# Dividing the softmax of an eight-head attention at the heads' outputs instead of at the probabilities

## The chip, the cores and the metric

The kernel runs on one core of one Trainium2 chip. A time is the device time of one execution in microseconds (us). The time before is the median of three runs; one more execution was recorded by the hardware profiler, and its rows and chains are what the text quotes. The engines are PE (TensorE: matmuls; its weight loads are listed as PEld), DVE (VectorE), ACT (ScalarE), POOL (GpSimd) and SP (SyncE, whose queue issues the DMAs here). Each takes its instructions in the order in which the program lists them, and waits at an instruction until what it needs is there.

## What is computed

64 graphs of 256 nodes with 256 features go through two layers. The first is two graph-attention steps, a layer norm, a feed-forward block of width 1024 with ReLU, and a second layer norm. The second layer is an attention with 8 heads of 32 features, a layer norm, a feed-forward block of width 1024 with GELU, and a layer norm. The change touches the attention of the second layer:

```python
scores = jnp.einsum('bhid,bhjd->bhij', q, k) / np.sqrt(dh)
attn = jax.nn.softmax(scores, axis=-1)
for r in range(Wv.shape[0]):          # R = 4 relations
    v_r = (src @ Wv[r] + bv[r])...    # per head
    mask = (adj_matrix == r)[:, None]
    out = out + jnp.einsum('bhij,bhjd->bhid', attn * mask, v_r)
attn_out = out.transpose(0, 2, 1, 3).reshape(Bb, Nn, Dm) @ Wo + bo
x = _ln(src + attn_out, g1, beta1)
```

The adjacency holds only zeros and ones, so two relations occur. The kernel uses the values of relation 0 for all pairs and the difference of the values of relation 1 and relation 0 for the pairs whose adjacency is one. All data is 32-bit floating point.

## The kernel before

Nothing of the 64 graphs is shared but the weights, which stay in SBUF. The work on one graph is cut into some 190 pieces, each a few instructions on one engine. Three lists written out in the source fix the order in which the program emits them: START, then PERIOD once per period (59 times), then END. An entry of PERIOD such as `A.dt13/3` means: piece A.dt13 of the graph that lies 3 behind the newest one. So six graphs are in work at a time, each in another stage, and each engine's stream is the list, filtered for its pieces. The scheduler of the framework is switched off for the five engines. It still adds the waits that the data and the buffers need.

The pieces that matter here, by their names in the lists. A letter ahead of the point is the stage: G graph attention, F first feed-forward and projections, A attention, T the tail with the second feed-forward.

- PE: G.wh0, G.wh1 (L747), G.eA, G.eB (L763), G.gA0, G.gA1 and G.gB (L800); F.ha to F.he and T.ha to T.he, the first product of each feed-forward block, done with seven products of blocks in place of eight (L661); F.f0, F.f1 (L686); T.fa to T.fe (L702), again seven products; F.q, F.k (L835); A.va to A.ve, the values (L848); A.sc0, A.sc1, the scores of four heads each (L880); A.o0, A.o1, the outputs of four heads each (L930); T.wo (L949).
- DVE: A.mx, the maxima of the scores (L887); A.rz, the reciprocals of the sums, 128x2 per head (L902); A.pm, the masked copy of the probabilities (L922); A.vk2, A.vk3 (L862), which take values out of PSUM and add a bias; G.away, the mask of the first layer, the first reader of the adjacency (L739); G.adA, G.adB, maxima in the first layer (L776 to L779); G.rzA, G.rzB, which divide the first layer's rows (L791, L794: whz); .ln, .nm and T.rbD, the layer norms (L502 to L538); F.hp1 to F.hp3 and T.hp1 to T.hp3, additions of PSUM to the hidden values (L637); T.fk1 to T.fk4 (L713) and T.fp1 to T.fp3 (L637), the same for the results.
- ACT: A.ex, the exponentials with their sums over a row (L894); G.wc, G.wd, G.lr, G.ex; F.r0 to F.r3 and T.ge0 to T.ge3, the activations (L678); F.qe, F.ke; A.vk1, A.vk4; A.oc0, A.oc1, which copy the outputs of four heads each from PSUM to oT and add the bias of the values (L941).
- POOL: A.sp, two scalings per head, of the probabilities by the reciprocals (L907); .ra and .rb, the weighted residuals (L554, L561); F.sA, F.sB, T.sC, sums of blocks for the seven products, and T.u0 to T.u3 (L584); .rs, the roots of the variances (L514).
- SP: L.xT, L.adj, L.x load a graph; T.out stores one.

A 32-bit tile is turned (transposed) in three steps, eleven times per graph: for each of eight heads' probabilities and for three layer norms. `.dt` is a transpose by DMA of the tile seen as 16-bit halves (L469, into one of two `pairs` buffers). `.dm` is two DMAs that bring the halves of the words together (L477, into one of two `halves` buffers). Then a copy joins the halves to words again (L484): `A.mg` for a head, F.cA, F.cB and T.cC for the norms. Of the eight joins of the heads POOL does the first head of each group of four, ACT does the other six, and ACT does the three of the norms. A new `.dt` waits until the `.dm` two turns back has landed, and a new `.dm` waits until the join two turns back has read its buffer.

So one head goes this way: scores on PE; maximum on DVE; exponentials and sums on ACT; reciprocal on DVE; scaling on POOL; transpose and halves by DMA; join on POOL or ACT; mask on DVE; outputs on PE:

```python
def over_sums(h):                                   # POOL, L904
    p = t["p", h]
    for i in range(NT):
        nc.gpsimd.tensor_scalar(
            p[:, :, :, i, :], p[:, :, :, i, :], t["rz", h][:, i : i + 1], 1.0,
            ALU.mult, ALU.mult,
        )
```

PSUM is handed out as eight banks of one kind to whoever comes next in the list. A second function, `general`, computes the same for adjacencies with other numbers; its instructions stand in the program behind a branch that these inputs don't take.

Of the kernel before, what the change touches and what calls it, by code (L numbers as in the profile page):

```python
# [25 lines left out]
F32 = mybir.dt.float32  # L26
U8 = mybir.dt.uint8
U16 = mybir.dt.uint16
# [6 lines left out]
P = 128  # L35
# [8 lines left out]
G.nmA/1 A.mx13/3 A.rz12/3 F.raB/4 F.sB/3 T.hk3/5 A.mx11/3 A.rz10/3 L.xT/0 T.hp3/5 A.vp2/4 A.dm02/4  # L44
A.pm03/4 G.wh0/0 A.mg02/4 T.hd/5 A.ex13/3 T.hp2/5 G.wh1/0 A.ex11/3 A.sp12/3 A.dm00/4 G.wc0/0
A.sp10/3 G.wc1/0 A.ve/4 A.pm01/4 F.dtA/1 A.mg00/4 F.dmA/1 F.f1/2 A.pm02/4 G.eA/0 A.pm00/4 T.rbC/5
F.rbB/4 A.vk4/4 T.he/5 T.ge0/5 A.rz11/3 A.pm11/4 A.rz13/3 A.dt10/3 F.lnB/2 A.sc0/3 A.o0/4 T.ge1/5
A.mx00/3 G.lrA/0 F.cA/1 T.hk4/5 A.o1/4 T.ge2/5 A.sp11/3 A.sp13/3 A.mx02/3 A.dt12/3 F.ha/1 A.oc0/4
T.ge3/5 L.adj/0 A.oc1/4 F.sA/1 A.ex00/3 F.hb/1 A.mx03/3 G.away/0 A.dm10/3 A.dm12/3 F.rsB/2 F.hk1/1
F.hk2/1 T.wo/4 A.mx01/3 G.adA/0 A.mg10/3 T.u0/5 F.hp1/1 T.lnC/4 F.hc/1 T.u1/5 A.mg12/3 A.dt13/3  # L50
G.exA/0 F.raA/1 A.dt11/3 F.nmB/2 A.ex03/3 A.dm13/3 G.rzA/0 T.fa/5 F.hk3/1 A.ex02/3 T.rsC/4 T.fb/5
F.hd/1 T.nmC/4 G.gA0/0 T.u3/5 T.fk1/5 T.fk2/5 A.rz03/3 A.ex01/3 T.u2/5 F.hp2/1 L.x/0 F.hp3/1
A.mg13/3 A.sp03/3 G.gA1/0 A.pm12/3 G.wd0/0 G.wd1/0 A.dm11/3 A.rz01/3 T.fc/5 A.va/3 A.vb/3 F.dtB/2
T.fk3/5 A.mg11/3 F.rbA/1 A.sp01/3 F.r0/1 A.pm13/3 T.dtC/4 A.rz02/3 A.vk1/3 G.eB/0 T.fd/5 F.dmB/2
T.fp1/5 A.vk2/3 G.lrB/0 T.fp2/5 F.cB/2 F.he/1 A.vc/3 T.dmC/4 T.fe/5 A.rz00/3 F.r1/1 G.adB/0
A.dt03/3 T.cC/4 A.dt01/3 F.q/2 A.vk3/3 G.exB/0 F.hk4/1 A.vp3/3 T.fp3/5 F.qe0/2 F.k/2 A.sp02/3
T.fk4/5 F.r2/1 T.ha/4 F.qe1/2 A.dm03/3 F.ke0/2 T.hk1/4 T.lnD/5 G.rzB/0 T.nmD/5 A.sp00/3 T.sC/4
G.gB/0 A.vp1/3 T.hb/4 A.dm01/3 T.rsD/5 A.dt02/3 T.raC/4 F.ke1/2 T.rbD/5 T.hp1/4 A.sc1/2 T.out/5
A.dt00/3 G.lnA/0 A.mg03/3 T.hk2/4 F.r3/1 A.mg01/3 A.mx12/2 A.mx10/2 A.vd/3 G.rsA/0 T.hc/4 A.pm10/3
F.f0/1 A.ex12/2 A.ex10/2  # L60
# [5 lines left out]
G.away:0 L.adj:2 S.lw:0 S.v0:0 L.adj:1 G.wh0:0 G.wh1:0 G.wc0:0 G.wc1:0 G.eA:0 G.lrA:0 G.adA:0  # L66
S.f0:0 G.exA:0 G.rzA:0 G.gA0:0 G.gA1:0 G.wd0:0 G.wd1:0 S.f1:0 G.eB:0 G.lrB:0 S.f2:0 L.xT:1 G.wh1:1
G.adB:0 G.wh0:1 L.xT:2 G.exB:0 G.rzB:0 G.wc0:1 G.wc1:1 G.gB:0 G.wh0:2 G.eA:1 G.away:1 G.lrA:1
G.lnA:0 G.rsA:0 G.nmA:0 G.adA:1 F.dtA:0 F.raA:0 G.exA:1 S.p2:0 S.v1:0 G.wh1:2 S.q0:0 G.wc0:2
G.rzA:1 G.wc1:2 G.gA0:1 G.gA1:1 L.xT:3 G.eA:2 G.wd0:1 F.dmA:0 S.v2:0 S.q1:0 G.wd1:1 G.eB:1 F.cA:0  # L70
G.lrB:1 F.sA:0 G.adB:1 G.lrA:2 L.x:1 F.ha:0 S.lr:0 F.hk1:0 F.hb:0 G.away:2 G.adA:2 F.hk2:0 F.hc:0
F.hk3:0 F.hp3:0 F.hd:0 F.hp2:0 G.exB:1 F.he:0 F.r0:0 F.hp1:0 G.wh1:3 G.rzB:1 S.j1:0 G.gB:1 G.lnA:1
F.r1:0 F.hk4:0 F.r2:0 F.r3:0 G.wh0:3 F.f0:0 G.wc0:3 G.exA:2 L.adj:3 G.rsA:1 G.nmA:1 G.rzA:2 F.f1:0
G.gA0:2 F.rbA:0 G.gA1:2 F.lnB:0 G.wd0:2 L.x:2 L.xT:4 G.wc1:3 S.v3:0 G.wh1:4 G.wd1:2 F.rsB:0
F.dtA:1 F.dmA:1 G.eA:3 G.eB:2 G.lrB:2 F.cA:1 F.nmB:0 G.wh0:4 G.adB:2 G.lrA:3 F.ha:1 F.sA:1 G.exB:2
F.hb:1 F.dtB:0 F.hk1:1 F.raB:0 G.rzB:2 G.away:3 F.dmB:0 F.hk2:1 G.gB:2 G.lnA:2 G.wc0:4 F.cB:0
F.hc:1 F.k:0 G.adA:3 G.rsA:2 G.wc1:4 G.nmA:2 F.hk3:1 F.ke0:0 F.q:0 F.ke1:0 F.hp3:1 F.hd:1 F.qe0:0
L.x:3 F.hp1:1 F.hp2:1 F.qe1:0 F.r0:1 A.sc1:0 F.raA:1 A.mx13:0 F.he:1 A.mx10:0 F.r1:1 A.ex13:0
F.dtA:2 F.hk4:1 F.rbB:0 F.raA:2 F.r2:1 A.sc0:0 F.r3:1 A.rz13:0 A.mx12:0 A.mx00:0 A.sp13:0 F.dmA:2
G.exA:3 A.ex10:0 A.ex12:0 A.mx01:0 A.ex01:0 A.dt13:0 A.rz10:0 G.rzA:3 A.rz12:0 F.cA:2 F.sB:0  # L80
F.f0:1 F.f1:1 G.gA0:3 A.sp10:0 F.rbA:1 A.dm13:0 A.mx02:0 A.ex02:0 A.mg13:0 A.dt10:0 A.rz01:0
A.ex00:0 G.wd0:3 G.gA1:3 A.sp12:0 F.lnB:1 A.dt12:0 A.va:0 A.vb:0 A.mx11:0 G.wd1:3 A.sp01:0 F.rsB:1
A.vk1:0 G.eB:3 A.dm10:0 A.dm12:0 A.mg10:0 F.nmB:1 G.lrB:3 F.dtB:1 A.ex11:0 A.mg12:0 A.mx03:0
S.l0:0 F.ha:2 F.hk1:2 A.rz00:0 A.dt01:0 G.adB:3 A.pm10:0 A.rz11:0 F.sA:2 A.vk2:0 F.dmB:1 A.rz02:0
F.hb:2 F.hk2:2 A.dm01:0 A.vc:0 F.hc:2 A.ex03:0 S.l1:0 A.vk3:0 A.pm13:0 A.vd:0 F.cB:1 A.sp11:0
A.rz03:0 F.k:1 G.exB:3 A.vp1:0 F.hk3:2 A.mg01:0 A.sp02:0 F.ke0:1 F.hp1:2 G.rzB:3 F.hp3:2 F.q:1
A.dt11:0 F.rbA:2 A.vp2:0 F.ke1:1 F.hd:2 A.ve:0 F.qe0:1 F.qe1:1 A.dt02:0 A.dm11:0 A.sp00:0 F.hp2:2
G.gB:3 A.pm12:0 A.dm02:0 A.vk4:0 A.sp03:0 G.lnA:3 S.l2:0 A.mg11:0 F.he:2 F.r0:2 A.sc1:1 G.rsA:3
A.mx11:1 F.hk4:2 A.mg02:0 A.mx12:1 A.vp3:0 A.ex11:1 A.sc0:1 F.r1:2 A.dt03:0 A.rz11:1 A.mx13:1
# [1223 lines left out]
```

## Time and profile before

| what | us |
|---|---|
| runs | 3124.27, 3115.12, 3122.83 |
| median | 3122.83 |
| profiled execution, own time | 3121.47 |
| its span, first to last instruction | 3119.7 |
| busy PE, DVE, ACT, POOL | 3007.0, 2747.0, 2548.7, 2290.2 |

The profiled execution's own time holds 1.8 us around its span. The granted TensorE clock is 0.992 of full speed in the mean and 1.00 from 500 to 3000 us. The 16 DMA engines are busy for 0.71 of the steady stretch in the mean, and nearly all their packets come from SP's queue.

How to read the rows: a group of instructions is given by its line in the source, engine, operation, out<-in, shapes and count; then the time in which any of them ran, and the mean time of one in ns; then the engine's idle time just before them, and what ended it. Instructions of one engine overlap a little, so the sum of single times is more than the busy time. A matmul of 32-bit numbers is two instructions in the trace. A wait row reads: engine and tile that waited, what it waited for, us in total, times, longest. "SPq" is the queue of SP, whose time to issue a DMA isn't counted as busy.

### The profile page before, as it was taken

The page shows a single profiled execution, that of the slowest core. Times are in us where ns is not written, and L with a number is a line of the kernel's source. Part 1 is how long each engine was busy: PE and PEld are TensorE (multiplying, and loading weights), DVE is VectorE, ACT ScalarE, POOL GpSimd, SP SyncE. Part 2 cuts the span into 40 slices and gives each one's busy share as a digit, 9 for nine tenths or more (in the row PEclk, how much of TensorE's full clock was granted, in tenths as well). Part 3 has the DMA queues.
Part 4 walks back from the last instruction along what each step waited for, and adds up shares of the span by engine and source line. Part 5 has one row for each costly group of instructions (what it writes and reads, how often), then busy time and mean ns, then how long its engine had stood idle before and what let it go on. Part 6 is the DMA issues. An engine that isn't in the chain of part 4 may idle for free.

```text
span 3119.7 us, 68789 instructions
## 1 busy us (share of the span) xinstructions
PE 3007.0 (96%) x23270; PEld 2629.7 (84%) x23270; DVE 2747.0 (88%) x5744; ACT 2548.7 (82%) x5822; POOL 2290.2 (73%) x3057
## 2 busy tenths in 40 slices
PE   6899999999999999999999999999999999999986
PEld 5788888888888888888898888888888888888876
DVE  5689999899998899898999899999999999889965
ACT  2688888888888888888888888888888888878874
POOL 4568777777777777777777777777777777777765
PEclk9999999999999999999999999999999999999998
DMA  5577766677676777776676666677677776767663
GB/s 156 108 145 149 149 149 143 146 155 143 149 151 137 142 146 151 148 152 138 155 150 144 148 142 145 150 152 147 147 153 145 149 149 143 146 138 151 149 133 73
DMA packets 1023941, 449.41 MB, mean 144 GB/s; under 512 B 771008, under 2 KB 1021888, under 8 KB 1023584
## 3 DMA queue, kind: packets, MB, share of 16 engines
q1 hardware_dynamic: 1022320, 442.70, 67.9%
q8 instruction: 188, 3.08, 0.5%
q0 software_dynamic: 976, 1.72, 0.4%
q14 instruction: 169, 1.38, 0.2%
q10 hardware_dynamic: 288, 0.52, 0.1%
HBM read 58.87 MB, written 16.78 MB: 24 GB/s over the span
## 4 chain that ended last, share of the span: by engine, by line
PE 68%; DVE 12%; DMA 8%; issue 3%; ACT 3%; POOL 1%; SPq 1%; DVEq 0%; ACTq 0%; POOLq 0%
PE ff_a L686 11%; PE hX_c L661 6%; PE o L930 5%; PE fX_c L702 5%; PE hX_a L661 4%; PE sc L880 3%; PE q L835 3%; PE hY_c L661 3%; PE k L835 3%; PE gat_b L800 3%; PE vX L848 3%; PE wh L747 3%; DVE pm L922 2%; PE wo L949 2%; DMA adj<-in_adjT 2%
## 5 line engine op out<-in xcount | busy, mean ns | idle before, releaser
L484 ACT COPY pm<-halves_p 128x1024 uint16<-128x1024 uint16 x384 | 522.4, 1360 | 137.8 <-DMA halves_p<-pairs_p 135.7
L922 DVE TENSOR_TENSOR pm<-pm,adj 128x512 f32<-128x512 f32 x512 | 565.6, 1123 | 19.3 <-POOL pm L484 12.2
L686 PE MATMUL ff_a<-w_L_gnn_w_ff,hid_a 128*128 128x256 f32 x2048 | 463.0, 379 | 0.1
L686 PEld LDWEIGHTS ff_a<-w_L_gnn_w_ff,hid_a 128*128 128x128 f32 x2048 | 384.0, 190 | 50.4 <-ACT hid_a L678 0.8
L484 POOL COPY pm<-halves_p 128x1024 uint16<-128x1024 uint16 x128 | 180.2, 1408 | 157.5 <-DMA halves_p<-pairs_p 140.4
L930 PE MATMUL o<-pm,v 128*32 128x256 f32 x4096 | 235.3, 381 | 5.5 <-POOL p L907 2.4
L678 ACT ACTIVATE hid_a<-hid_a,col_L_gnn_b_ff 128x256 f32<-128x256 f32 x512 | 230.1, 500 | 3.3 <-DVE hid_a L637 3.2
L678 ACT ACTIVATE hid_c<-hid_c,col_L_gnn_b 128x256 f32<-128x256 f32 x512 | 224.4, 498 | 5.1 <-DVE hid_c L637 2.4
L930 PEld LDWEIGHTS o<-pm,v 128*32 128x32 f32 x4096 | 126.2, 110 | 104.6 <-issue 15.9
L702 PE MATMUL fX_c<-f_L_gnn_W,hid_c 128*128 128x128 f32 x1536 | 207.2, 278 | 7.3 <-ACT hid_c L678 5.1
L514 POOL TENSOR_TENSOR rstd_a<-var_a,neghalf 128x2 f32<-128x2 f32 x64 | 45.0, 702 | 222.5 <-DVE var_a L510 222.5
L702 PEld LDWEIGHTS fX_c<-f_L_gnn_W,hid_c 128*128 128x128 f32 x1536 | 192.8, 192 | 13.2 <-ACT hid_c L678 5.8
L661 PEld LDWEIGHTS hX_a<-cols_a,f_L_gnn_w_ff 128*128 128x128 f32 x1024 | 126.9, 195 | 33.1 <-ACT hid_c L678 22.2
L880 PE MATMUL sc<-kT,qT 32*128 32x256 f32 x2048 | 149.6, 400 | 3.3 <-ACT p L894 2.8
L584 POOL TENSOR_TENSOR S_c<-cols_c 128x128 f32<-128x128 f32 x128 | 58.3, 455 | 128.4 <-ACT cols_c L484 128.4
L800 PE MATMUL gat_a<-whz_A,s_A 128*128 128x258 f32 x512 | 134.9, 400 | 18.2 <-DVE whz_A L794 15.4
L661 PE MATMUL hX_a<-cols_a,f_L_gnn_w_ff 128*128 128x128 f32 x1024 | 144.6, 285 | 6.4 <-ACT cols_a L484 5.0
L747 PE MATMUL wh<-wx,xT 128*128 128x260 f32 x512 | 136.0, 390 | 12.5 <-DVE wx L372 10.1
L661 PEld LDWEIGHTS hX_c<-S_c,f_L_gnn_W 128*128 128x128 f32 x1024 | 134.0, 191 | 8.5 <-ACT hid_c L672 1.3
L702 PE MATMUL fY_c<-f_L_gnn_W,H_c 128*128 128x128 f32 x1024 | 137.3, 278 | 3.8 <-POOL H_c L584 3.8
L661 PE MATMUL hX_c<-cols_c,f_L_gnn_W 128*128 128x128 f32 x1024 | 135.8, 276 | 2.7 <-ACT cols_c L484 2.7
L661 PE MATMUL hX_a<-S_a,f_L_gnn_w_ff 128*128 128x128 f32 x1024 | 136.9, 277 | 0.0
(2760 smaller groups left out, 9808.9 us busy)
## 6 DMA issues: line engine op xcount, KB each, us to landing
halves_p<-pairs_p SPq DMA_DIRECT2D x1024, 128.0 KB, 3.3
xT<-in_xT SPq DMA_DIRECT2D x64, 256.0 KB, 3.4
adj<-in_adjT SPq DMA_DIRECT2D x64, 256.0 KB, 3.5
x<-in_x SPq DMA_DIRECT2D x64, 256.0 KB, 3.5
halves_y_a<-pairs_y_a SPq DMA_DIRECT2D x128, 128.0 KB, 3.0
halves_y_y<-pairs_y_y SPq DMA_DIRECT2D x128, 128.0 KB, 3.5
halves_y_c<-pairs_y_c SPq DMA_DIRECT2D x128, 128.0 KB, 3.2
out<-res_d SPq DMA_DIRECT2D x64, 256.0 KB, 2.6
```

The source lines that it names most:

```text
L484: copy(into().bitcast(U16).rearrange("p (n s) -> p s n", s=2), t["halves"].rearrange("p s k q -> p s (k q)"),)
L661: nc.tensor.matmul(ps[:, f * P : (f + 1) * P], weights()[0][:, factor, f * P : (f + 1) * P], left, start=start and f == 0, stop=f == FC // ...
L678: nc.scalar.activation(tiles["hid"][:, f, :], tiles["hid"][:, f, :], func, bias=b1[:, f : f + 1])
L686: nc.tensor.matmul(tiles["ff"][:, i, :], tiles["hid"][:, f, nodes(i)], weights()[2][:, f, :], start=(f == 0), stop=(f == FC - 1),)
L702: nc.tensor.matmul(ps, left[:, f, :], weights()[2][:, factor, f * P : (f + 1) * P], start=start and f == 0, stop=f == FC // 2 - 1, skip_gr ...
L747: nc.tensor.matmul(t["whp", j], tiles["xT"][:, c, nodes(j)], wx[:, c, :], start=(c == 0), stop=(c == KC - 1),)
L800: nc.tensor.matmul(ps, t["s"][:, j, nodes(i)], t["whz"][:, j, :width], start=(j == 0), stop=(j == NT - 1),)
L835: nc.tensor.matmul(t[key + "p"][:, o, :], w[:, c, nodes(o)], tiles["cols"][:, c, :], start=(c == 0), stop=(c == KC - 1),)
L848: nc.tensor.matmul(ps, left, wv[:, factor, :], start=start, stop=True, skip_group_check=True)
L880: nc.tensor.matmul(t["sc", g, hh][:, i, :], qkv["q"][hd, g, nodes(i)], qkv["k"][hd, g, :], start=True, stop=True,)
L922: nc.vector.tensor_tensor(pm[:, 1, :], pm[:, 0, :], tiles["adj"], ALU.mult)
L930: nc.tensor.matmul(ps[hh * DH : (hh + 1) * DH, :], qkv["v"][:, j, d0 : d0 + DH], t["pm", (g, hh)][:, r, j * N : (j + 1) * N], start=(r == ...
```

## The change

The probabilities stay undivided. They are turned, joined and masked as the exponentials come, and the outputs of the heads are multiplied by the reciprocals of the sums when they are taken out of PSUM. There the nodes lie along the free dimension, so the reciprocals are needed as rows, the same row in all 32 partitions of a head. They get there in five new pieces: A.iz (DVE) takes the reciprocals of all sums of a graph at once, four times side by side, so that a tile of 128x64 words, or 128x128 16-bit halves, is full; A.zt (SP) turns this tile by DMA; A.zd (SP) stores 32 of its rows in DRAM, 256 bytes each; A.zr (SP) reads them back in four DMAs, each spreading one row of 2 KB over 32 partitions; A.zj (ACT) joins the halves to words.

The pieces A.rz (DVE) and A.sp (POOL) are gone. A.oc0 and A.oc1 move from ACT to DVE and become a product with these rows. The bias of relation 0's values, which they added, is multiplied by the output weights once, in the setup (S.w1, four matmul instructions), and added to a bias row that is added to the residual anyway (S.w2). Four joins of heads instead of two are done on POOL. The buffers of p (the probabilities) become three instead of four, those of the first layer's scores s one instead of two. All three lists are new.

```diff
-t["z", h] = small.tile([P, NT], F32, tag="az", name=f"az_{b}_{g}{hh}", bufs=4)
-p = t["p", h] = work.tile([P, 2, NT, NT, 64], F32, tag="p", name=f"p_{b}_{g}{hh}", bufs=4)
+if "z" not in t:
+    t["z"] = small.tile([P, HG, HEADS // HG, NT], F32, tag="az", name=f"az_{b}", bufs=2)
+p = t["p", h] = work.tile([P, 2, NT, NT, 64], F32, tag="p", name=f"p_{b}_{g}{hh}", bufs=3)
...
-def inverse(h):
-    t["rz", h] = small.tile([P, NT], F32, tag="arz", name=f"arz_{b}_{h}", bufs=8)
-    nc.vector.reciprocal(t["rz", h], t["z", h])
...
+def inverses():
+    t["rz"] = small.tile([P, 4, HEADS * NT], F32, tag="arz", name=f"arz_{b}", bufs=1)
+    z = t["z"].rearrange("p h g i -> p (h g i)")
+    nc.vector.reciprocal(t["rz"], z.unsqueeze(1).to_broadcast([P, 4, HEADS * NT]))
+def turn_inverses():
+    t["zrow"] = work.tile([P, P], U16, tag="zrow", name=f"zrow_{b}", bufs=1)
+    nc.sync.dma_start_transpose(
+        out=t["zrow"], in_=t["rz"].rearrange("p a n -> p (a n)").bitcast(U16)
+    )
+def store_inverses():
+    t["flat"] = dram.tile([HG, 2 * HEADS // HG * NT, P], U16, tag="flat", name=f"flat_{b}", bufs=2)
+    nc.sync.dma_start(out=t["flat"].rearrange("h k q -> (h k) q"), in_=t["zrow"][: 2 * HEADS * NT])
+def spread_inverses():
+    t["zs"] = work.tile([P, HEADS // HG * NT, 2, P], U16, tag="zs", name=f"zs_{b}", bufs=1)
+    for hh in range(HG):
+        nc.sync.dma_start(
+            out=t["zs"][hh * DH : (hh + 1) * DH].rearrange("p k s q -> p (k s q)"),
+            in_=t["flat"][hh].rearrange("k q -> (k q)").partition_broadcast(DH),
+        )
+def join_inverses():
+    t["inv"] = work.tile([P, HEADS // HG, N], F32, tag="inv", name=f"inv_{b}", bufs=1)
...
+    copy(words.rearrange("p (k q s) -> p k s q", k=HEADS // HG * NT, s=2), t["zs"])
...
-nc.scalar.activation(
-    t["oT"][:, g, :], t["op", g], AF.Identity, bias=bv0[:, g : g + 1], scale=1.0
-)
+nc.vector.tensor_tensor(t["oT"][:, g, :], t["op", g], t["inv"][:, g, :], ALU.mult)
...
-    partial(both, h), "POOL" if hh in ((0,), (0,))[g] else "ACT",
+    partial(both, h), "POOL" if hh in ((0, 2), (0, 2))[g] else "ACT",
...
-s = t["s"] = work.tile([P, NT, N], F32, tag="s", name=f"s_{step}{b}", bufs=2)
+s = t["s"] = work.tile([P, NT, N], F32, tag="s", name=f"s_{step}{b}", bufs=1)
```

The new PERIOD, whose order the prediction walks through:

```
A.dm10/4 A.mg10/4 L.xT/0 A.zj/4 T.hp2/5 T.ge0/5 A.pm02/4 T.he/5 F.dmA/1 A.pm10/4 F.lnB/2 A.sc0/3
A.o0/4 T.raC/5 F.cA/1 A.mx10/3 A.o1/4 A.mx03/3 A.mx00/3 T.ge1/5 F.rsB/2 A.oc0/4 A.mx01/3 T.hk4/5
A.dt13/3 A.dt12/3 F.sA/1 T.rbC/5 G.wh0/0 T.ge2/5 L.adj/0 A.oc1/4 T.ge3/5 A.dm13/3 A.ex00/3
A.dm12/3 A.ex01/3 G.wh1/0 G.wc0/0 G.away/0 A.mg12/3 G.wc1/0 F.ha/1 G.eA/0 F.hb/1 A.dt11/3 T.u0/5
A.mx02/3 A.mg13/3 F.nmB/2 G.lrA/0 F.hk1/1 F.hk2/1 T.wo/4 A.ex03/3 A.dt00/3 G.adA/0 T.lnC/4
A.ex10/3 F.raB/3 G.exA/0 A.dm11/3 T.u1/5 A.dm00/3 T.fb/5 A.mg00/3 F.hc/1 T.fa/5 F.hk3/1 A.mg11/3
F.hd/1 G.rzA/0 A.dt03/3 F.hp3/1 F.dtB/2 A.ex02/3 T.fk1/5 F.hp1/1 G.gA0/0 T.rsC/4 G.gA1/0 G.wd0/0
T.nmC/4 A.dm03/3 G.wd1/0 T.fk2/5 A.va/3 F.dmB/2 T.fp1/5 A.vk1/3 A.vb/3 F.hp2/1 T.dtC/4 G.eB/0
T.u3/5 G.lrB/0 F.rbB/3 T.fc/5 A.iz/3 F.he/1 F.cB/2 A.mg03/3 A.vk2/3 T.fk3/5 T.u2/5 G.adB/0 F.raA/1
A.vc/3 T.fd/5 A.vp1/3 A.dt01/3 F.r0/1 L.x/0 T.fp2/5 G.exB/0 T.dmC/4 A.pm11/3 F.k/2 A.vk3/3 F.q/2
T.fe/5 F.hk4/1 A.zt/3 G.rzB/0 A.pm00/3 A.dm01/3 F.ke0/2 T.cC/4 F.ke1/2 F.r1/1 A.vd/3 A.vp3/3
F.r2/1 F.qe0/2 F.rbA/1 T.fp3/5 A.dt02/3 T.sC/4 T.fk4/5 A.zd/3 A.dt10/3 T.lnD/5 G.gB/0 F.qe1/2
A.vp2/3 T.ha/4 T.rsD/5 T.hb/4 A.ve/3 G.lnA/0 T.hk1/4 A.sc1/2 T.hk2/4 T.hc/4 F.r3/1 G.rsA/0 T.nmD/5
A.vk4/3 T.rbD/5 A.dm02/3 A.zr/3 G.nmA/0 A.mg01/3 F.sB/2 F.f0/1 A.mg02/3 A.mx13/2 A.ex13/2 T.hp1/4
T.hk3/4 T.hd/4 F.f1/1 A.mx12/2 A.mx11/2 T.out/5 A.pm03/3 A.pm13/3 A.pm01/3 A.ex12/2 A.ex11/2
F.dtA/0 A.pm12/3 T.hp3/4
```

In the old one the neighbours of the same places on DVE's and SP's side are: T.hp2 directly behind T.hd and ahead of A.pm01, A.pm02, A.pm00 and F.lnB; L.adj behind A.dt12; T.lnC, F.nmB and G.rzA between T.wo and G.gA0.

## The prediction

> **What bounds the kernel now.** I first read the busy times, then a steady stretch, the starts of one matmul group from graph to graph, the waits, and the rows of what the change touches.
>
> The page's busy times of the whole execution:
>
> ```profile
> PE 3007.0 (96%) x23270; PEld 2629.7 (84%) x23270; DVE 2747.0 (88%) x5744; ACT 2548.7 (82%) x5822; POOL 2290.2 (73%) x3057
> ```
>
> The same in the steady stretch, where start and end don't dilute it:
>
> ```profile
> core 0: us, PE busy (x) PEld busy (x) DVE busy (x) ACT busy (x) POOL busy (x), PEclk, DMA share, GB/s
> 200.00:2900.00 2700.00, 2661.89 (x20866) 2335.65 (x20856) 2469.22 (x5138) 2296.79 (x5246) 2035.74 (x2707) 1.00 0.71 147
> ```
>
> PE is busy for 98.6% of it, at the full clock. Two key groups of consecutive graphs, in the timeline of PE (start, duration):
>
> ```profile
> 1489.28 1.89 PE L835 MATMUL k<-cols_y,w_L_gnn_Wk 128*128 128x256 f32 x8
> 1534.94 1.89 PE L835 MATMUL k<-cols_y,w_L_gnn_Wk 128*128 128x256 f32 x8
> ```
>
> They lie 45.66 us apart. From graph 5 to 58 the distance is 46.90 us in the mean, and never under 45.66. Adding up PE's groups of one period, each by the shortest usual distance to the next group, gives 45.65: that is **PE's floor**, and a period loses 1.25 us over it. 2700 us are 57.6 periods, so per period PE is busy 46.2, DVE 42.9 (idle 4.0), ACT 39.9, POOL 35.4. DVE is the second bound. The waits (us in total, times, longest) say the same:
>
> ```profile
> DVE hid_c L637 <- PE hX_c L661: 68.9, 60, 3.0
> ...
> DVE away L739 <- DMA adj<-in_adjT: 64.3, 44, 3.6
> ...
> PE gat_a L800 <- DVE whz_A L794: 15.4, 25, 2.7
> ...
> PE fX_c L702 <- DVE acc_c L713: 12.0, 34, 1.1
> ```
>
> What PE waits for most in the steady state is DVE being late (whz, then the sums after it in DVE's order), and DVE is late because it waits twice a period, about 1.1 us each, for PE's hX_c and for the adjacency's landing.
>
> **The change, part by part.** The rows of what is moved:
>
> ```profile
> L484 ACT COPY pm<-halves_p 128x1024 uint16<-128x1024 uint16 x384 | 522.4, 1360 | 137.8 <-DMA halves_p<-pairs_p 135.7
> ...
> L484 POOL COPY pm<-halves_p 128x1024 uint16<-128x1024 uint16 x128 | 180.2, 1408 | 157.5 <-DMA halves_p<-pairs_p 140.4
> ...
> L941 ACT ACTIVATE oT<-o,col_bv 128x256 f32<-128x256 f32 x128 | 60.0, 471 | 46.5 <-PE o L930 46.0
> ```
>
> PE: the same matmuls per graph; four instructions once in the setup. The floor stays 45.65.
>
> POOL: 16 scalings of L907 go. They are 551.6 us in the stretch, 9.6 a period. Two joins come, 2 x 1.41. Net -6.8: 35.4 becomes 28.6. POOL sets no end, so this is worth nothing by itself; its cover was 11 us of spare time.
>
> ACT: two joins and two copies of the outputs go, the join of the inverses comes (1024 16-bit elements, as L484): -2 x 1.36 - 2 x 0.47 + 1.36 = -2.3. ACT has 7 us spare; nothing by itself.
>
> DVE: eight reciprocals go. L902 has 69.3 us for 460, 0.15 each, but in DVE's timeline the next instruction starts 0.07 later, so the gain is 0.6 to 1.2. Two products at the heads' outputs come; the nearest row is L862 (128x256, one side in PSUM), 0.41, so 0.8. One reciprocal of 128x64 comes, which no row shows: between 0.15 (128x2) and 0.68 (the maximum of 128x512, L887); I take 0.25, nearest to the 0.28 of 128x128 (L713). Sum -0.4 to +0.9, taken +0.3. Against it stands DVE's contention with POOL. DVE's timeline:
>
> ```profile
> 1362.68 4.04 DVE L922 TENSOR_TENSOR pm<-pm,adj 128x512 f32<-128x512 f32 x3
> 1366.65 0.15 DVE L902 RECIPROCAL arz_(1, 1)_16112<-az 128x2 f32<-128x2 f32 x1
> 1366.72 0.66 DVE L922 TENSOR_TENSOR pm<-pm,adj 128x512 f32<-128x512 f32 x1
> ```
>
> The three mask products of the first line take 1.35 each, with POOL in its additions L561 (in POOL's timeline from 1362.71 to 1366.18). The one of the last line takes 0.66; a scaling L907 starts beside it only at 1366.90. Another, which started after a scaling, took 0.94 (at 1360.20). With fewer scalings and more joins I take 0.3 back: DVE's busy time **stays at 42.9**. The Trainium skill (SBUF — State Buffer, "Who interferes with whom") says that a DVE instruction with two SBUF inputs contends with any GpSimd instruction that reads SBUF. Scaled by POOL's time (35.4 to 28.6), the 3.5 us a period that the masks lose would shrink by 0.7, and the forecast by 40 us; the 0.66 beside a scaling that started later says that only some overlaps cost DVE.
>
> SP and the DMAs: 37 issues of 30.3 us per period today. The change adds a transpose (1.26 to issue), a store and four spreads (0.59 each): +4.2. Landings, from issue:
>
> ```profile
> halves_p<-pairs_p SPq DMA_DIRECT2D x1024, 128.0 KB, 3.3
> ...
> out<-res_d SPq DMA_DIRECT2D x64, 256.0 KB, 2.6
> pairs_p<-p SPq DMA_TRANSPOSE x512, 3.2
> ```
>
> SP is nearly a ring: two `pairs` buffers, so a transpose waits for the landing of the halves two turns back. Walking through SP's order with these figures alone I get 41.5 us before and 41.9 after: the added issues mostly fill time in which SP waits for landings. Not free, but under 45.65. Store and spread in this form are in no row: I bound a landing by 2.2 (shortest `out`) and 6.6 (longest `halves_p`) and take 2.6 and 3.3, the medians of the nearest rows.
>
> Smaller edits: p with three buffers is covered, since the scaling that held it is gone; s with one costs nothing, as its uses follow each other on PE; the bias at L941 goes into a row once.
>
> **The order.** I laid PE's new order out back to back, T.he at 0: o0 2.1, o1 3.8, wo 10.4, gA0 17.5, k 25.2, gB 30.1 to 31.8, T.hd 41.3, f1 42.2 to 45.65.
> - T.hp2 (hid_c) now stands behind F.f1 instead of straight behind T.hd, so DVE's wait of 1.1 goes. In its place T.he needs hp2: from gB's end DVE has 14 pieces of 14.4 us, about 13.4 with their overlap, for 13.7 available. Late next: the mask products there, if POOL's additions run beside them.
> - whz for gA0: from hp2 17.9 of DVE's work, 16.8 with overlap, before 17.5; 0.7 spare, where it is overdrawn now.
> - The outputs' products: o1 ends at 5.7, DVE comes to oc1 at about 7, wo starts at 10.4. Hidden; if DVE is over 3 us late, T.wo waits, and behind oc0 and oc1 queue away, nmB and adA.
> - The adjacency stays behind a transpose that waits for landings, so I keep its 1.0.
> - **New wait, w**: SP's order is turn of inverses, halves, turn, store, turn, halves, spread, out, dtA, dm10. From mg03 (about 26.6, behind cB) I get the store at 31.7, the spread at 35.4 to 37.8, dm10 at 39.7, landed 43.6, joined on POOL by 45.0. DVE wants pm10 at about 46. That is 1 us spare by medians, with four landings in series, any of which can be 1 us or more late. I take w = 0.4 in the mean.
>
> Sum: DVE 42.9 busy + 4.0 idle - 1.1 + 0.4 = 46.2 a period, 0.55 over PE's floor: 0.7 less than 46.9. PERIOD runs 59 times: 41 us. The profiled execution took 3121.5 (span 3119.7), 1.4 under the median of the three runs, 3122.8: 3121.5 - 41 = **3080**. Start and end I take as unchanged: the last graph trades the scaling (about 1.2) for a chain of landings that lies beside its last heads' own.
>
> **Rivals.** *All of PE's loss goes*: w and the adjacency's wait vanish since SP has slack. 59 x 1.25 = 74: 3048. For it: a third of the periods already run within 0.5 us of the floor. Against: landings vary.
> *The freed time is where nobody waits*: POOL and ACT have 7 to 11 us spare already, DVE's wait moves to pm10 or to T.he. 3121.
> *Slower, by SP*: the spread can't be issued until the store has landed, and dtA and dm10 queue behind it; then mg10, pm10, and with pm10 PE's o1 and DVE's lnB are late. Each us that dm10's chain is late beyond its 1 us spare is a us of w; from w = 1.1 the gain is gone. At w = 1.6, if the landings average 0.7 us over the medians, the period is 47.4: 3121.5 + 59 x 0.5 = 3151. For it: SP's ring is within 4 us of the period. Against: the transposed tile is small, an eighth of the others. The Trainium skill (DMA: Bandwidth & Descriptors, "Specifications") says that under 512 bytes a DMA does a read-modify-write; the store's rows are 256 bytes. No run here shows one.
>
> **How the numbers follow.** Forecast 3080: 0.38. Floor, 3048: 0.19. No change, 3121: 0.16. Slower, 3151: 0.27. A difference of 0.3% (9 us) is about what can be told from no change. So faster 0.57, same 0.16, slower 0.27. The range takes in the floor case and reaches to the slower one: 3042 to 3152.
>
> **What would show it.** Right: distances of k near 46, DVE's wait for hX_c gone, POOL busy about 28.6 and ACT 37.6 a period, no PE wait at o, T.he or wo. Wrong: PE waiting at o for pm, or at T.he for hid_c; SP waiting long for flat or zrow; the reciprocal over 0.7; DVE busy over 44.

## The result and the profile after

Four runs of the changed kernel took 3149.78 to 3166.07 us, median **3158.15**; the kernel before, beside it on the same chip, 3115.12 to 3130.01, median 3123.55. The ratio is **1.0112** (95% interval 1.0075 to 1.0149): slower by 1.1%, where 3080 was forecast, and above the range's end of 3152. The profiled execution took 3154.8 us, its span is 3153.0.

The span is 33.3 us longer. PERIOD's 59 turns, from the first PE piece of PERIOD to the first of END, took 2762.3 us before and 2791.4 after (46.82 and 47.31 each); START and END are 2.2 and 2.1 us longer. So 29 of the 33 us came in the period, where 41 were forecast to go. From graph 5 to 58 two key groups lie 47.27 us apart in the mean, 46.90 before.

The busy times of the whole execution, and those of the steady stretch (columns as in the prediction):

```profile
PE 3008.8 (95%) x23274; PEld 2615.6 (83%) x23274; DVE 2627.9 (83%) x5425; ACT 2424.5 (77%) x5632; POOL 1861.0 (59%) x2161
```

```profile
200.00:2900.00 2700.00, 2635.67 (x20675) 2303.78 (x20676) 2317.31 (x4795) 2163.09 (x5035) 1629.89 (x1885) 1.00 0.77 152
```

The matmuls are the same (but for four in the setup) and the clock is 1.00, yet PE did less in the stretch: it waits longer. POOL, ACT and DVE all have less to do than before; 2700 us are now 57.1 periods, so DVE is busy for 40.6 us of a period (before 42.9), ACT 37.9, POOL 28.5. The busy share of the DMA engines rose from 0.71 to 0.77. The waits (engine, tile, what it waited for: us in total, times, longest):

```profile
PE vY L852 <- DVE acc_c L641: 57.9, 57, 1.9
...
PE gat_a L804 <- DVE whz_A L798: 7.6, 6, 4.0
...
PE fX_c L706 <- DVE acc_c L717: 5.1, 1, 5.1
```

The two waits of PE that the prediction showed have shrunk (from 15.4 and 12.0). In their place stands one that is there in nearly every period: the second value matmuls, A.vb, wait 1.0 us for T.fp1 on DVE, though they don't read its result: it frees the PSUM bank that they take. Why it is late, in the timelines of DVE, PE and POOL (start, duration, in brackets the idle time before):

```profile
1487.12 2.63 DVE L523 TENSOR_SCALAR y_c<-acc_c,mv_c,rstd_c 128x256 f32<-128x256 f32 x2 [0.48 <-POOL rstd_c L518]
1489.67 0.28 DVE L717 TENSOR_TENSOR acc_c<-fY_c,res_c 128x128 f32<-128x128 f32 x1
1489.87 0.27 DVE L641 TENSOR_TENSOR acc_c<-acc_c,fZ_c 128x128 f32<-128x128 f32 x1
```

```profile
1490.20 0.70 PE L852 MATMUL vY<-f_Wv,S_y 128*128 128x256 f32 x2 [0.59 <-DVE acc_c L641]
```

```profile
1484.98 1.47 POOL L488 COPY pm<-halves_p 128x1024 uint16<-128x1024 uint16 x1 [2.05 <-DMA halves_p<-pairs_p]
1486.39 0.69 POOL L518 TENSOR_TENSOR rstd_c<-var_c,neghalf 128x2 f32<-128x2 f32 x1
1487.06 1.26 POOL L588 TENSOR_TENSOR H_c<-hid_c,H_c 128x512 f32<-128x512 f32 x1
```

T.fp1 (1489.87) stands behind T.nmC (1487.12), which waits for T.rsC on POOL (1486.39), and that stands in POOL's order behind the join A.mg00 (1484.98), which had itself waited 2.05 us for the landing of its halves. T.nmC then runs for 2.63 us beside POOL's additions.

That is the wait which the profile shows. A second one it shows only on SP. Its timeline over most of a period (`x2` of L473 and `x4` of L481 are neighbours drawn together):

```profile
1491.49 1.25 SPq L473 DMA_TRANSPOSE pairs_y_c<-y_c  x1
1492.83 1.29 SPq L473 DMA_TRANSPOSE pairs_p<-p  x1
1494.17 0.59 SPq L327 DMA_DIRECT2D x<-in_x  x1
1494.86 1.20 SPq L481 DMA_DIRECT2D halves_y_c<-pairs_y_c  x2
1496.11 1.24 SPq L914 DMA_TRANSPOSE zrow<-arz  x1
1497.45 1.19 SPq L481 DMA_DIRECT2D halves_p<-pairs_p  x2
1498.73 1.26 SPq L473 DMA_TRANSPOSE pairs_p<-p  x1
1500.04 0.58 SPq L920 DMA_DIRECT2D flat<-zrow  x1
1501.22 1.23 SPq L473 DMA_TRANSPOSE pairs_p<-p  x1
1502.56 1.20 SPq L481 DMA_DIRECT2D halves_p<-pairs_p  x2
1503.81 2.84 SPq L926 DMA_DIRECT2D zs<-flat  x4
1506.69 0.42 SPq L1018 DMA_DIRECT2D out<-res_d  x1
1508.55 1.27 SPq L473 DMA_TRANSPOSE pairs_y_a<-y_a  x1
1509.91 1.20 SPq L481 DMA_DIRECT2D halves_p<-pairs_p  x2
```

From 1491.5 to 1507.1 one issue follows the other almost without a gap, the turn (L914), the store (L920) and the spreads (L926) among them. The gap before 1501.22 ends when the halves issued at 1497.45 land, the one before 1508.55 with the landing of those issued at 1502.56.

I compared, for each of SP's pieces in 48 periods, its start with the end of the issue before it, with the landing it needs (of its transpose for `.dm`, of the halves two turns back for `.dt`) and with the end of the engine that writes its data, and sorted SP's time by which came last:

| us of a period | period | issuing | a landing last | an engine last | short gaps |
|---|---|---|---|---|---|
| before | 46.90 | 30.8 | 13.0 | 1.8 | 1.2 |
| after | 47.27 | 34.6 | 10.5 | 0.6 | 1.6 |

**SP hardly waits for any engine.** Its own issues, their landings and the short gaps between fill 46.7 of 47.3 us (45.0 of 46.9 before): a ring with almost no slack, into which the change put 3.8 us of issues.

### The profile page after: what moved, and what is told of

Read it like the earlier page. It is cut to its first block, busy times and chain, and to the rows that moved or that the text cites. A ratio compares the mean times of both kernels' runs of the same rounds, so it can differ in the third digit from the quotient of the medians.

```text
span 3153.0 us, 67189 instructions
## 1 busy us (share of the span) xinstructions
PE 3008.8 (95%) x23274; PEld 2615.6 (83%) x23274; DVE 2627.9 (83%) x5425; ACT 2424.5 (77%) x5632; POOL 1861.0 (59%) x2161
## 4 chain that ended last, share of the span: by engine, by line
PE 53%; DMA 15%; DVE 14%; ACT 7%; POOL 4%; issue 4%; SPq 2%; POOLq 0%; DVEq 0%; ACTq 0%
DMA halves_p<-pairs_p 9%; PE ff_a L690 8%; PE fX_c L706 5%; PE hX_c L665 5%; PE o L957 4%; PE hX_a L665 3%; PE q L839 3%; PE k L839 3%; DVE y_c L523 3%; PE gat_b L804 3%; POOL pm L488 3%; PE sc L884 3%; PE wh L751 2%; DMA pairs_p<-p 2%; PE hY_c L665 2%
## 5 line engine op out<-in xcount | busy, mean ns | idle before, releaser
L488 POOL COPY pm<-halves_p 128x1024 uint16<-128x1024 uint16 x256 | 350.5, 1369 | 551.5 <-DMA halves_p<-pairs_p 518.2
L949 DVE TENSOR_TENSOR pm<-pm,adj 128x512 f32<-128x512 f32 x512 | 389.6, 794 | 49.9 <-POOL pm L488 48.4
L488 ACT COPY pm<-halves_p 128x1024 uint16<-128x1024 uint16 x256 | 347.0, 1355 | 9.7 <-DMA halves_p<-pairs_p 9.4
L523 DVE TENSOR_SCALAR y_c<-acc_c,mv_c,rstd_c 128x256 f32<-128x256 f32 x128 | 157.2, 1268 | 34.4 <-POOL rstd_c L518 34.4
L488 ACT COPY cols_a<-halves_y_a 128x1024 uint16<-128x1024 uint16 x64 | 86.4, 1349 | 101.5 <-DMA halves_y_a<-pairs_y_a 101.3
L665 PEld LDWEIGHTS hX_c<-cols_c,f_L_gnn_W 128*128 128x128 f32 x1024 | 134.3, 192 | 14.2 <-ACT cols_c L488 4.8
L665 PE MATMUL hX_a<-cols_a,f_L_gnn_w_ff 128*128 128x128 f32 x1024 | 137.6, 277 | 6.0 <-ACT cols_a L488 2.9
L775 ACT ACTIVATE s_B<-e_B,wh_B 128x256 f32<-128x256 f32 x128 | 53.7, 471 | 116.4 <-PE e_B L767 116.4
L852 PE MATMUL vY<-f_Wv,S_y 128*128 128x256 f32 x256 | 84.4, 412 | 61.2 <-DVE acc_c L641 57.9
```

The source lines that it names most:

```text
L488: copy(into().bitcast(U16).rearrange("p (n s) -> p s n", s=2), t["halves"].rearrange("p s k q -> p s (k q)"),)
L523: nc.vector.tensor_scalar(y[:, :, :, i, :], tiles["acc"][:, i, :].rearrange("p (k c d) -> p c k d", k=KC, c=2), tiles["mv"][:, i, 0:1], ti ...
L665: nc.tensor.matmul(ps[:, f * P : (f + 1) * P], weights()[0][:, factor, f * P : (f + 1) * P], left, start=start and f == 0, stop=f == FC // ...
L852: nc.tensor.matmul(ps, left, wv[:, factor, :], start=start, stop=True, skip_group_check=True)
L949: nc.vector.tensor_tensor(pm[:, 1, :], pm[:, 0, :], tiles["adj"], ALU.mult)
```

## The experiments

Theory 1 was the wait of A.vb, theory 2 (the prediction's slower rival) SP's chain, theory 3 the two joins moved to POOL. All ratios are to the kernel before, run beside it on the same chip, with their 95% intervals; "period" is the mean distance of the key groups from graph 5 to 58. The runs are spread over five chips, on which the kernel before took 3123 to 3137 us, so periods and times of different chips differ by up to 0.4% for that alone; the ratios don't.

**1. T.fp1 early.**

```diff
 T.fk1/5
+T.fp1/5
 F.hp1/1
...
 T.nmC/4 A.dm03/3 G.wd1/0 T.fk2/5 A.va/3 F.dmB/2
-T.fp1/5
```

> One entry of the period's order is moved: T.fp1 of the last stage, which takes a result out of PSUM on VectorE, stands directly behind T.fk1 again, ahead of T.nmC and T.fk2; everything else is the changed kernel. Theory 1 (PE's second value matmuls, A.vb, wait 0.96 us a period for the PSUM tile that T.fp1 frees, because T.fp1 stands behind T.nmC, which is late and slow): the wait at the value matmuls (57.9 us in the whole trace) goes to under 10, the period falls from 47.3 to about 46.4, and the time from 3158 to about 3105. Theory 2 (SyncE's chain of turn, store and spread sets the period): the order on SyncE is untouched, so 3158 within 10. Theory 3 (the two further joins on GpSimd): 3158 within 10, since the joins stay.

Ratio 1.0086 (1.0056 to 1.0116), period 47.45. The wait of 57.9 us is gone, and nothing is gained. Others came, on PE and on ACT:

```profile
PE hX_a L664 <- ACT p L898: 22.2, 31, 1.6
PE vX L851 <- ACT p L898: 21.6, 25, 3.1
```

```profile
ACT p L898 <- DMA pairs_p<-p: 115.6, 78, 3.7
```

The last row is 73.5 in the changed kernel, and before the change it was:

```profile
ACT p L894 <- DMA pairs_p<-p: 7.9, 7, 3.3
```

ACT's exponentials wait for one of the three buffers of p, which is free when the turn of an older head has landed; PE's matmuls wait for the PSUM banks that the exponentials empty. Theory 1 alone falls.

**2. T.rsC early.**

```diff
+T.rsC/4
 A.mg00/3 F.hc/1 T.fa/5
...
-T.rsC/4
```

> One entry moved: T.rsC, a small GpSimd piece that VectorE's T.nmC waits for, stands ahead of the join A.mg00 instead of behind F.hd; T.nmC and T.fp1 stay where they are. Theory 1: T.nmC no longer waits (0.5 us a period), but still runs beside GpSimd's additions at 1.27 us a piece, so only a part of the wait of the value matmuls goes: period about 46.9, time about 3130 (3115 to 3145). Theory 2: 3158 within 10. Theory 3: 3158 within 10.

Ratio 1.0091 (1.0064 to 1.0119). A.vb's wait fell to 15.0 us, the time stayed: a miss of the same kind.

**3. Without the chain of the inverses.**

```diff
-A.iz A.zt A.zd A.zr A.zj
-nc.vector.tensor_tensor(t["oT"][:, g, :], t["op", g], t["inv"][:, g, :], ALU.mult)
+nc.vector.tensor_tensor(t["oT"][:, g, :], t["op", g], late["inv"][:, g, :], ALU.mult)
```

> The reciprocal, its turn, its store, its spread and its join on ScalarE are left out; the heads' outputs are multiplied by a constant tile instead, so they are not divided by their sums. The order of all other pieces stays. Theory 1: the wait at the value matmuls is untouched but for the 0.5 us of the reciprocal, which stands behind A.vb; time 3145 to 3160. Theory 2 (SyncE's chain holds the other transfers): the chain is gone, so the time falls below 3130.

Ratio 1.0037 (1.0021 to 1.0052), which is 3135 us where the kernel before takes 3123.55, between the two expectations. Period 47.16; SP now waits for engines 3.1 us a period, most of it before the store of the results, so its ring is no longer the limit, and A.vb's wait is the largest of PE's that is left. PE's and SP's rows:

```profile
PE vY L849 <- DVE acc_c L638: 59.3, 56, 2.0
```

```profile
SPq L1013 <- DVE res_d L537: 141.8, 60, 4.3
```

**4. Two joins on POOL instead of four.**

```diff
-partial(both, h), "POOL" if hh in ((0, 2), (0, 2))[g] else "ACT",
+partial(both, h), "POOL" if hh in ((0,), (0,))[g] else "ACT",
```

> GpSimd joins one head of each group, as before the change, and ScalarE the other three; the orders stay those of the change. Theory 1: the join A.mg00, which stands ahead of T.rsC, stays on GpSimd, so the wait stays; ScalarE gets 2.8 us a period more and has the room: 3158 within 12. Theory 3 (the further joins are the cause): the time falls to 3125 or below.

Ratio 1.0121 (1.0092 to 1.0149): no gain. A run that leaves the other two suspects in place can't clear the joins by itself; run 5 does, which keeps all four on POOL and is faster than the kernel before. Theory 3 falls with that.

Theory 4 came out of these: two limits of nearly one height, so that either cure alone leaves the other.

**5. Both out:** the edits of runs 1 and 3.

> The first and the third experiment in one: T.fp1 directly behind T.fk1, and the reciprocal, its turn, store, spread and join left out, so that the heads' outputs are multiplied by a constant tile and not divided by their sums. Theory 4, made after the first four runs: two limits of nearly one height, the wait of the value matmuls (47.1 us a period when SyncE is relieved) and SyncE's own ring of issues and landings (47.4 when T.fp1 is early), so that either alone brings little; with both gone the period falls to about 46.3 and the time to some 1.5% under the kernel before (ratio 0.985). Rival: the first experiment lost what it gained for another reason (ScalarE's order, or the clock); then the ratio stays at 1.004 or above.

Ratio **0.9903** (0.9878 to 0.9927), period 46.38. Together they bring 2.1%, where alone they brought 0.3% and 0.8%. The size is less than the 1.5% under before that I expected. The steady stretch:

```profile
200.00:2900.00 2700.00, 2675.01 (x21038) 2347.76 (x21037) 2390.34 (x4827) 2131.21 (x5066) 1671.44 (x1920) 1.00 0.75 148
```

PE fits 1.8% more matmuls into the stretch than after the change (21038 to 20675). Theory 4 holds. The edit of run 3 takes out the reciprocal on DVE and its join on ACT too, and no run takes out these two alone; runs 13 and 14, which keep both, show most of the gain. Runs 6 to 16 and 18 ask what in the chain costs SP, and whether a cure exists that keeps the computation; all have T.fp1 early.

**6 and 7. Store and spreads issued by another engine:** ACT in run 6, POOL (`nc.gpsimd`) in run 7.

```diff
-nc.sync.dma_start(out=t["flat"].rearrange("h k q -> (h k) q"), in_=t["zrow"][: 2 * HEADS * NT])
+nc.scalar.dma_start(out=t["flat"].rearrange("h k q -> (h k) q"), in_=t["zrow"][: 2 * HEADS * NT])
```

> The full computation: T.fp1 directly behind T.fk1, and the store of the turned inverses and the four spreads issued by ScalarE instead of SyncE, at the same places of the order. Theory 4: SyncE loses 2.6 us of issues and two waits a period, ScalarE gets the issues (at most 3 us a period, with 8 us free); period 46.3 to 46.6, ratio to the kernel before 0.985 to 0.995. Rival (the added transfers cost by their landings and their load on the DMA engines, not by SyncE's issues): ratio 1.005 to 1.01, as with T.fp1 early alone.

> As the run with ScalarE as issuer, but GpSimd issues the store and the spreads. Theory 4: the same gain, ratio 0.985 to 0.995, if GpSimd's issues cost no more than SyncE's; if they are dear (GpSimd also writes the descriptors), T.sC and the join A.mg02 behind them come later, and it is between that and 1.009.

By ACT 1.0081 (1.0057 to 1.0105), no gain over run 1; by POOL 1.0242 (1.0214 to 1.0270). With ACT, SP's issues fell to 31.8 us, but its waits for landings rose to 12.9, and ACT stood idle for 1.2 us ahead of A.mg01, behind the spreads. That was not for the store: it had landed 2.6 us (median) before the first spread was issued. In this program the DMAs of SP and ACT take turns on eight semaphores, and each waits until the last one on its semaphore has landed. The fourth spread started within 0.1 us after such a landing, of a transfer of SP, in 45 of 48 periods. Where SP issues the whole chain, the last one on a semaphore landed at least 1.0 us before the next issue on it, so there it costs nothing. So the runs with ACT as issuer (6, 9, 11, 12, 16, 18) changed two things at once. With POOL, which waited 54 us in all for the store, A.mg02 behind the spreads started 3.2 us later than in run 1, counted from the key group.

**8. T.fp1 and T.rsC early:** the edits of runs 1 and 2.

> T.fp1 directly behind T.fk1 and T.rsC ahead of the join A.mg00; the computation is complete. Theory 4: the wait of the value matmuls is gone, SyncE's ring is not, so nothing is gained over either move alone: ratio 1.005 to 1.01. Rival (VectorE's lateness at T.nmC is what counts): ratio under 1.

Ratio 1.0096 (1.0072 to 1.0121), as theory 4 says.

**9. The turn on ACT's queue too,** beside the edit of run 6.

```diff
-nc.sync.dma_start_transpose(
+nc.scalar.dma_start_transpose(
     out=t["zrow"], in_=t["rz"].rearrange("p a n -> p (a n)").bitcast(U16)
```

> The full computation: T.fp1 early, and all of the chain (turn, store, spreads) issued by ScalarE, at the same places. Theory 5, made after the runs with the store and the spreads off SyncE: SyncE's ring is a row of landings (a transpose waits for the halves of two turns back), and only an issue that stands where SyncE would not wait anyway lengthens it. The turn does (1.25 us, between the halves of T.dmC and A.dm01, whose data have landed); the store and the spreads stand mostly in waits. So with the turn off SyncE too the period falls to about 46.5: ratio 0.990 to 0.996. Rival (the transfers cost by load on the DMA engines or as transposes among transposes, whoever issues them): ratio 1.005 to 1.01 as before.

Ratio 1.0312 (1.0281 to 1.0343): much worse. SP's next transpose now waits for the landing of the turn on the other queue, which took 4.6 us from issue in place of 2.8:

```profile
SPq L472 <- DMA zrow<-arz: 157.7, 63, 3.8
```

So this run says nothing of issue against transfer: the two queues' transposes came one after the other. The order is the program's: SP's transpose waits at the semaphore of ACT's.

**10. Three loads moved into SP's waits.**

```diff
 A.dm10/4
-L.xT/0
 F.dmA/1 A.dt13/3
+L.xT/0 L.adj/0
 A.dt12/3
-L.adj/0
 A.dm13/3
...
 F.dmB/2
+L.x/0
 T.dtC/4 A.dt01/3
-L.x/0
```

(Here and in run 15 only SP's pieces are shown.)

> The full computation, the chain on SyncE as in the changed kernel, T.fp1 early; three loads are moved on SyncE to where it waits for a landing: L.xT and L.adj directly behind A.dt13, L.x behind F.dmB. Nothing is taken off SyncE. Theory 5: the loads stood, 0.6 us each, where SyncE would not have waited; the ring loses about 1.8 us, more than the 1.3 of the turn: period 46.4 to 46.7, ratio 0.988 to 0.998. Rival (SyncE's issues as such, or the DMA load): no change against T.fp1 early alone, ratio 1.005 to 1.01.

Ratio 1.0278 (1.0249 to 1.0307). My theory 5, that only an issue outside of SP's waits costs, is not borne out; it left out what the moved loads do to the landings beside them. The transpose A.dt12, now right behind the loads, lands after 4.5 us (3.3 in run 1), the halves A.dm13 after 4.8 (4.0): the loads, of 256 KB each, were in flight beside them. L.adj also started 0.6 us later than SP could, just as the mask A.pm10, which still reads the old adjacency, ended.

**11 and 12. The edits of runs 9 and 10 together, and T.rsC early as well.**

> Both: the chain issued by ScalarE and the three loads moved, T.fp1 early, the computation complete. Theory 5: SyncE's ring is well under PE's floor; the period is what PE and VectorE leave, 46.1 to 46.4, ratio 0.983 to 0.992. Rival: 1.0 or above.

> As the run with both cures, with T.rsC ahead of the join A.mg00 as well. If VectorE's wait at T.nmC counts once SyncE is out of the way, 0.1 to 0.3 us a period less than without (ratio 0.002 to 0.006 lower); if PE has slack there, no change.

Ratios 1.0442 (1.0411 to 1.0473) and 1.0447 (1.0416 to 1.0478): the two losses nearly add up.

**13 and 14. The chain in halves.** In 13 the turn is left out, and the store reads a constant tile; in 14 the store and the spreads, and the join reads one.

```diff
-A.zt
-in_=t["zrow"][: 2 * HEADS * NT])
+in_=late["zrow"][: 2 * HEADS * NT])
```

```diff
-A.zd A.zr
-words.rearrange("p (k q s) -> p k s q", k=HEADS // HG * NT, s=2), t["zs"]
+words.rearrange("p (k q s) -> p k s q", k=HEADS // HG * NT, s=2), late["zs"]
```

> T.fp1 early, and only the turn of the inverses left out: the store takes its rows from a constant tile written once (so the outputs are divided by a constant, not by their sums), the reciprocal, store, spreads and join stay. If the turn is what lengthens SyncE's ring: period 46.4 to 46.7, ratio 0.990 to 0.997. If the store and the spreads do it, by their issues or as load: ratio 1.005 to 1.01, as with T.fp1 early alone. In between, if each has a share.

> The counterpart: T.fp1 early, the turn stays, the store and the four spreads are left out, and the join takes a constant tile (outputs divided by a constant). If the turn lengthens the ring: ratio 1.004 to 1.009, as with these transfers issued by ScalarE. If the store and the spreads do it: 0.990 to 0.997.

Ratios 1.0018 (0.9999 to 1.0038) and 0.9991 (0.9975 to 1.0007), periods 47.02 and 46.87. From run 1 (1.0086) the turn is worth 0.7%, the store with the spreads 0.95%, all of the chain (run 5) 1.8%: **each part has its share**: 0.43 us a period for the turn (1.25 us of issues), 0.58 for the rest (2.6 us); the periods are from different chips.

**15 and 16. The turn moved into a wait,** with the whole computation; 16 has the store and the spreads on ACT.

```diff
 T.dtC/4
+A.zt/3
 A.dt01/3
-L.x/0
 T.dmC/4
-A.zt/3
+L.x/0
 A.dm01/3
```

> The full computation, T.fp1 early; on SyncE the turn is moved from between T.dmC and A.dm01 to directly behind T.dtC, where SyncE waits for that transpose's landing, and the load L.x from there to the place behind T.dmC. If the turn's issue is the cost: A.dm01 starts 0.6 us earlier, ratio 0.995 to 1.003. If it is the turn's transfer, which stands among the other transposes wherever it is issued: 1.005 to 1.012; then dt01 lands later by what the turn takes.

> As the run with the turn moved, and the store and the spreads issued by ScalarE. If issues are the cost: another 0.2 us a period, ratio 0.990 to 1.000. If transfers are: 1.004 to 1.012.

Ratios 1.0195 (1.0179 to 1.0211) and 1.0165 (1.0149 to 1.0181): worse. A.dt01 is issued some 1.5 us later, counted from the key group, its landing takes 3.7 us instead of 3.3, that of A.dm01, now behind L.x, 4.1 instead of 3.4. Neither place was free. In run 16 the spreads on ACT waited as in run 6.

**17. The chain's transfers added to the kernel before,** in its old order, without use (the spreads go to DRAM).

```diff
 T.dmC/4
+A.zt/3
 A.dt03/3 A.dt01/3 A.dm03/3
+A.zd/3
 A.dm01/3 A.dt02/3 T.out/5
+A.zr/3
 A.dt00/3
```

> The kernel before, with its order and its arithmetic, and the chain's transfers added without use: SyncE turns a constant tile behind T.dmC, stores it behind A.dm03 and spreads it with four transfers of the same size, into DRAM (there is no room left in SBUF), behind T.out. Outputs are unchanged. If SyncE's ring of issues and landings is what the chain costs, in the old order too (there SyncE waits 1.7 us a period for engines' data, the rest of its time is issues and landings): 0.3 to 1.2 us a period more, ratio 1.006 to 1.025. If the old order has the room that the prediction saw (ring 41.5 us): ratio under 1.004.

Ratio **1.0570** (1.0545 to 1.0594), period 49.39: more than twice what I expected. SP issues for 35.2 us (before 30.8), and its waits for landings fell by 2.0 only. PE waits for the load that stands behind:

```profile
PE wh L747 <- DMA xT<-in_xT: 86.1, 52, 7.2
```

So the old order had no room for the chain, at these places at least. The changed kernel, with the same transfers at other places, loses 1.1%: its other parts, the new order among them, give most of the 5.7% back; which of them was not tested.

**18. Run 6, with the spreads and the join of the inverses later.**

```diff
-A.zr/3
...
 A.ex11/2
+A.zr/3
...
-A.zj/4
 T.hp2/5 T.ge0/5
+A.zj/4
```

> As the run with the store and the spreads issued by ScalarE, but the spreads stand behind A.ex11, when the store has long landed, and the join of the inverses behind T.ge0: ScalarE no longer waits 1.2 us for the store ahead of A.mg01. If that wait ate what SyncE gained: period 46.8 to 47.0, ratio 0.999 to 1.004. If the transfers themselves lengthen the landings in SyncE's ring: 1.005 to 1.010, as before.

Ratio 1.0480 (1.0452 to 1.0507), and it doesn't tell what it was for. The store had landed long before the spreads, as meant, but the wait of run 6 was not for the store: the second to fourth spreads each started as the last transfer on their semaphore landed (0.02 us after it in the median), xT's load among these. ACT stood there and then at the join, T.ge0 and all exponentials behind came some 2.5 us later, and PE waited for them:

```profile
ACT L681 <- DMA xT<-in_xT: 205.9, 50, 6.3
```

```profile
PE hX_a L664 <- ACT p L898: 117.4, 60, 6.7
```

## Why the prediction was wrong

**The step that failed** is the one on SP: "Walking through SP's order with these figures alone I get 41.5 us before and 41.9 after: the added issues mostly fill time in which SP waits for landings. Not free, but under 45.65." SP's issues, landings and short gaps take 46.7 of 47.3 us, not 41.9. The walk was short already for the kernel before: 41.5, where the trace has 45.0, the period of 46.9 without the 1.8 us in which SP waited for engines. A walk that misses by 3.6 us should not have been used to judge 4 us of new issues.

What it left out shows when the walk is repeated. With the medians it took (3.2 for a transpose, 3.3 for the halves) it gives 41.8 before and 42.0 after, much as in the prediction. With the means, counted from the last issue (3.4 and 3.55, as single landings reach 5.3 and 6.6), it gives 44.1 for both; with the 0.06 us between two issues too, 44.8 and 45.2; and with each issue and landing as the trace of its run has it, 45.3 and 46.2. So some 0.2 us more for each landing, over eleven turns a period, is most of the miss. The last of these walks also gives 46.6 for run 1, 45.4 for run 3, 45.0 for run 5 and 48.2 for run 17: long where SP was taken to be the limit, short where it was not. (They hold no wait for an engine, and lie 0.9 to 1.8 us under the periods measured.)

"Mostly fill time in which SP waits" was right: of 3.8 us more issuing, 2.5 fell into waits for landings (13.0 to 10.5) and 1.2 into waits for engines (1.8 to 0.6). The room that the walk saw beyond these was not there. Run 17 shows the price in the old order: 2.5 us a period.

**The sum** "DVE 42.9 busy + 4.0 idle - 1.1 + 0.4" took DVE's time as the period. DVE's busy time fell by 2.3 us a period, and the period grew all the same; DVE is idle for 6.7 us of it now. So this sum was not the bound after the change.

**The order** was walked for five edges. A.vb behind T.fp1, T.nmC, T.rsC and A.mg00 was not among them. It costs 57.9 us of PE's time, but taking it away alone gains nothing (run 1); with the chain gone and this wait left the period is 47.16 (run 3).

**The buffers of p**: "covered, since the scaling that held it is gone". Not so: ACT waits 73.5 us for them, 7.9 before. But this wait is not by itself what makes the kernel slower, as run 5, the fastest, has it too:

```profile
ACT p L896 <- DMA pairs_p<-p: 70.4, 57, 3.3
```

Whether it comes from the three buffers or from the new order was not tested.

The terms, each measured:

- PE's floor 45.65: right, the shortest distance in run 5 is 45.67.
- POOL 28.6: 28.5. ACT 37.6: 37.9.
- The reciprocal, taken 0.25: 0.54 (row below), within its bounds. The products 0.42 each, as taken. (The lower end of that sum adds up to -0.25, not -0.4, which changes nothing.)
- DVE's contention, taken as 0.3 back: the eight masks fell from 1123 to 794 ns, 2.6 a period. The Trainium skill's rule (SBUF — State Buffer, "Who interferes with whom") would have given 0.7 by my scaling; the trace shows the direction that the rule says, and more of it. It was no help, as DVE was not the bound.
- T.hp2's wait: 68.9 to 17.5, as forecast. The adjacency's, which I kept: 64.3 to 4.7.
- The new wait w at pm10: 48.4 us in all, 0.8 a period, for 0.4; PE hardly waits at o. Nor does it at wo.
- Start and end: some 4 us longer, taken as unchanged.

```profile
L949 DVE TENSOR_TENSOR pm<-pm,adj 128x512 f32<-128x512 f32 x512 | 389.6, 794 | 49.9 <-POOL pm L488 48.4 <-ACT pm L488 1.5
...
L909 DVE RECIPROCAL arz<-az 128x64 f32<-128x64 f32 x64 | 34.6, 541 | 0.1
```

**The rivals.** "Slower, by SP" at 3151 was near the 3155 of the profiled execution, and had the right engine, but another mechanism: dm10 late past its 1 us, through w at 1.6. The store landed in 2.1 us and a spread in 2.7, earlier than taken. It is not one late landing; the ring as a whole is full.

What stays open: whether the store and the spreads cost by their issues or by what they put in flight. Leaving them out gains 0.95%, having ACT issue them nothing, but there ACT waits for semaphores that it shares with SP, and no run gave its DMAs semaphores of their own. A third `pairs` buffer, which might loosen the ring, wasn't tried. No run with the whole computation beat the kernel before; run 5, which leaves out the division, shows what is left at most for one that gets the inverses across without SP: about 1%, with the reciprocal and its join still to pay.

## What to carry to other kernels

Before giving an in-order DMA queue more to do, sort its present time in the trace by what came last at each issue: its own issue, a landing that it waits for, or an engine. Only the last part is room, and a paper walk counts only if it reproduces the period that is measured; where landings follow each other in series, walk with their means and not their medians. When DMAs move to another engine, look which semaphores they share: a wait that looks like one for data can be one for an unrelated landing. Where two chains have nearly the same length, removing either shows almost nothing: test them together before discarding one.

## What the runs showed of the hardware

- A transpose issued on a second queue while SP issues transposes landed after 4.6 us instead of 2.8, and SP's next transpose waited for it (run 9). The program orders them, by a semaphore; what they would do unordered no run shows.
- A store of 8 KB in rows of 256 bytes landed after 2.1 us, a spread of 64 KB after 2.7. The Trainium skill (DMA: Bandwidth & Descriptors, "Specifications") names a read-modify-write under 512 bytes; no run stores the same bytes in longer rows, so whether the 2.1 us hold a price of it isn't shown.
- T.nmC's scaling of 128x256 took 1268 ns in the mean, 873 before, with POOL's additions beside it in the turn shown above; y_a's, with the same shape, 550 and 697.
